# An early-fusion network with an LSTM on one core: output rows kept as (sequence, pair of steps), stored in rows of 2 KB

## The chip, the core and the metric

The kernel runs on one core of a Trainium2 chip. The metric is the device time of one execution in microseconds (us). A core has five engines that run at once and wait for each other on semaphores: TensorE (PE; its weight loads are shown apart as PEld), VectorE (DVE), ScalarE (ACT), GpSimd (POOL) and SyncE (SP). SP issues most transfers (queue q1 of the profile), ACT a few (q10), GpSimd the indirect ones (q0); all are carried out by the same 16 DMA engines. On-chip memory (SBUF) has 128 partitions; HBM is off the chip.

## The reference, cut to what matters

16 images become 441 tokens each, and 128 text tokens are appended: h has 16 sequences of 569 tokens of 256 numbers. Two layers follow. The second half of the second layer is what the change touches:

```python
h = h + _L1_attn_ref(_layernorm(h), ...)
h = h + _L1_ffn_ref(_layernorm(h), ...)

def _L1_ffn_ref(x, W_ih, W_hh, b_ih, b_hh, W_lin, b_lin, fw_att, bw_att):
    lstm_out = _lstm(x, W_ih, W_hh, b_ih, b_hh)        # 569 steps, 16 sequences, 256 units
    logits = lstm_out @ W_lin.T + b_lin
    g = argmax(logits, axis=-1)[..., None]             # 0 or 1 for each token
    w = g * lstm_out
    inc = jnp.cumsum(w, axis=1)                        # over the steps
    prefix = inc - w
    suffix = inc[:, -1:, :] - inc
    return 2.0 * lstm_out + prefix * fw_att + suffix * bw_att
```

Everything is float32. The output is (16, 569, 256): 9.32 MB, of which one token of one sequence is 1 KB. The suffix needs the total over all steps, which is known only after the last one.

## The kernel before, in words

**Stages.** First the tokenizer, the window attention and the routing (to about 900 us of the profile), then the experts of the mixture (to 1650), then layer 1. In layer 1 the attention of later tokens runs beside the recurrence of earlier ones (1650 to about 3250 us); then the recurrence runs alone (to 3443), and a tail follows.

**Order of the work.** The order on PE, DVE, ACT and POOL is fixed when the kernel is built. A planner (`Order.run`) takes streams of work, Python generators that yield an engine and an estimated time ("DVE+", 0.14 + ...) ahead of each instruction, and picks the next by these estimates; the recurrence (`steps`) is its chain and goes first. SP's transfers stand in the order in which the generators issue them. The change leaves all these estimates as they are.

**Rows between the attention and the LSTM.** `back` (L1390) ends each block of the attention by storing h into `HF` in HBM (L1489): one store for each sequence, 64 partitions of 1 KB for a block of 64 tokens. There are ten blocks (`BLOCKS`: 32 tokens, eight times 64, then 25). `HF[j]` is laid out (token, sequence, 256).

**The recurrence.** `steps` (L1576) does 569 steps. In each, TensorE adds W_hh times the state to the gates (L1637), ACT and DVE turn gates into the new state X (L1653 to L1680), which is kept with the units on the partitions: X is (128, 2 halves, step, sequence), its step 32 numbers apart because two copies of the 16 sequences stand side by side.

**The sums.** 37 runs (`RUNS`) of mostly 16 steps, then 8 and 1, go through `sums_of` (L1687) when their steps are done. It issues the load `hf` of the rows of h (L1692); computes the gate for all of a run's tokens (`fin`, L1700) and w (L1714) as (sequence, step); sums over the steps of each sequence by a scan (L1722, `sum`); makes `y`, laid out (step, sequence), from the sum, w and X in four DVE operations, two for each half of the units (L1729, L1734); turns y by TensorE so that tokens stand on the partitions (`turned`, L1743: eight steps x 16 sequences fill 128 partitions and make a unit; a run of 16 steps has two units); and adds hf (L1752). The sum goes to `PD` in HBM (L1757) as long as SBUF has no room, and later straight into `O`, an SBUF tile of (128, 72 units, 256), which first takes back what `PD` holds (L1789). So partition 16 t + b of O holds sequence b, and column u holds step 8 u + t.

**The tail.** The total of all steps, times bw_att, is spread over 128 partitions (L1797), turned (L1804) and copied to `T1` (L1806). T1 is added to all columns of O, in seven pieces of 2, 5, 8, 12, 14, 15 and 15 columns (L1810; L1815 for the last step alone). After each piece eight stores, one for each t, go out (L1818), in turn from SP and ACT: each reads 16 partitions, one for each sequence, and writes pieces of 1 KB that lie 8 KB apart in a sequence of the output.

Of the kernel before, what the change touches and what calls it, by code (L numbers as in the profile page):

```python
# [10 lines left out]
F32 = mybir.dt.float32  # L11
BF16 = mybir.dt.bfloat16
AF = mybir.ActivationFunctionType
ALU = mybir.AluOpType
# [3 lines left out]
D = 256  # L18
T = 569
# [30 lines left out]
BLOCKS = [(0, 32)] + [(32 + 64 * i, 64) for i in range(8)] + [(544, 25)]  # L50
STEPS = 8
UNITS_OF = [[(u, min(STEPS, n - u)) for u in range(0, n, STEPS)] for _, n in BLOCKS]

RUNS = []
# [228 lines left out]
def kernel(ctx: ExitStack, tc: tile.TileContext, a: dict, out: bass.AP):  # L283
    nc = tc.nc
    NB = out.shape[0]
# [3 lines left out]
    ident = const.tile([128, 128], F32, name="ident")  # L289
# [41 lines left out]
    dram = ctx.enter_context(tc.tile_pool(name="dram", bufs=1, space=bass.MemoryType.DRAM))  # L331
# [10 lines left out]
    before = route.tile([128, E, E], F32, name="before")  # L342
# [579 lines left out]


    HB = [dram.tile([128, D], F32, name=f"HB{p}") for p in range(NP)]
    HF = [dram.tile([n, NB, D], F32, name=f"HF{j}") for j, (_, n) in enumerate(BLOCKS)]

    XPD = [dram.tile([n, 2, NB, 512], F32, name=f"XPD{j}") for j, (_, n) in enumerate(BLOCKS)]
    PHD = dram.tile([128, 2, NP * 128], F32, name="PHD")
# [3 lines left out]
    ls = ctx.enter_context(tc.tile_pool(name="lstm", bufs=1))  # L932
# [14 lines left out]
    weights = ls.tile([128, 3, 2], F32, name="weights")  # L947
# [25 lines left out]
    with tc.tile_pool(name="lb", bufs=1) as lbp:  # L973
# [4 lines left out]
        v = lstm_b.rearrange("p (q r) -> p q r", r=128)[:, :, 64:96]  # L978
# [21 lines left out]
    def gate_columns(w, gate):  # L1000
        return w.rearrange("p (q r) -> p q r", r=128)[:, :, 32 * gate : 32 * gate + 32]

    for k in range(2):
        for gate in (0, 1, 3):
            v = gate_columns(Whh[:, k, :], gate)
# [5 lines left out]
    for v in (Wih[:, 0, :], Wih[:, 1, :]):  # L1011
        v = gate_columns(v, 2)
# [4 lines left out]
    for n in ("Wk2", "Wq2"):  # L1017
        t = l1w.tile([128, 2, 2, 64], F32, name=n)
# [10 lines left out]
    def bank(name, slot):  # L1029
        return ps.tile([128, 512], F32, name=name, tag=f"bank{slot}", bufs=1)  # L1030
# [359 lines left out]
    def back(p, c, batch, at, slot, late=False):  # L1390

        u = f"{p}_{c}_{late}"
# [6 lines left out]
        n = 1 if c8 else 2  # L1399
        block, r0, m = (len(BLOCKS) - 1, 0, 25) if late else (0, 32, 32) if c8 else (1 + c, 0, 64)  # L1400
# [8 lines left out]
        w = wk.tile([128, 2, 128], F32, name=f"w{u}", tag=f"w{slot}")  # L1409
# [22 lines left out]
        if c8:  # L1432
            h = wk.tile([128, n, D], F32, name=f"bh{u}", tag=f"bh{slot}")
            yield "at", ("kept", p, c)
            for j in range(2):
                for s in range(2):
                    b = 2 * j + s
# [5 lines left out]
        r = bank(f"r{u}", slot).rearrange("p (k n) -> p k n", k=2)  # L1443
# [16 lines left out]
        for k in range(2):  # L1460
            yield ("DVE/ACT", 0.34, 0.36) if c8 else ("DVE/ACT", 0.54, 0.46)
            src, to = tr[:, k, :], nT[:, k, :]
            if c8:
                src = src.rearrange("p (b x) -> p b x", x=64)[:, :, r0 : r0 + 32]
# [20 lines left out]
        for j in range(2):  # L1485
            for s in range(2):
                b = 2 * j + s
                src = h[32 * b : 32 * b + m, 0, :] if c8 else h[64 * s : 64 * s + m, j, :]
                nc.sync.dma_start(HF[block][:, 2 * p + b, :], src)  # L1489
        mv, rstd = yield from stats(h, f"d{u}", slot)  # L1490
        xn = yield from norm(h, mv, rstd, f"dxn{u}", slot)
        tr = yield from turn(xn, f"dtr{u}", slot, n)
# [3 lines left out]
        for i in range(2 * n):  # L1496
            j, half = i // 2, i % 2
# [74 lines left out]
    tail = {"stored": 0, "at": 0}  # L1572
# [114 lines left out]
    def sums_of(r, j, u, n, X):  # L1687


        m, units = NB * min(n, STEPS), -(-n // STEPS)  # L1690
        hf = ls.tile([128, 2, D], F32, name=f"hf{r}", tag="hf", bufs=3)
        nc.sync.dma_start(  # L1692
            hf[:m, :units, :],
            HF[j][u : u + n].rearrange("(i t) b d -> (t b) i d", i=units),
        )
        logit = ps.tile([128, 512], F32, name=f"fin{r}", tag="fin", bufs=1)
        logit = logit[:, : NB * n]
        for k in range(2):
            yield "PE", NB * n * COLUMN
            nc.tensor.matmul(  # L1700
                logit.rearrange("p (t b) -> p t b", b=NB), wl[:, k, :], X[:, k],
                start=(k == 0), stop=(k == 1),
            )

        w = ls.tile([128, 2, NB, n + 1], F32, name=f"w{r}", tag="w2", bufs=1)
        yield "ACT", 0.2
        if r:
            m_, before = sums[r - 1]
            nc.scalar.copy(w[:, :, :, 0], before[:, :, :, m_])
        else:  # L1710
            nc.scalar.activation(w[:, :, :, 0], X[:, :, 0, :], AF.Identity, scale=0.0)
        for k in range(2):
            yield "DVE", 0.14 + 0.002 * NB * n
            nc.vector.scalar_tensor_tensor(  # L1714
                w[:, k, :, 1:].rearrange("p b t -> p t b"),
                logit.rearrange("p (t b) -> p t b", b=NB), shut, X[:, k], ALU.is_gt, ALU.mult,
            )
        before = ls.tile([128, 2, NB, n + 1], F32, name=f"sum{r}", tag="sum", bufs=2)
        sums[r] = n, before
        for k in range(2):  # L1720
            yield "DVE+", 0.1 + 0.0025 * NB * (n + 1)
            nc.vector.tensor_tensor_scan(  # L1722
                before[:, k].rearrange("p b t -> p (b t)"), begins[n],
                w[:, k].rearrange("p b t -> p (b t)"), 0.0, ALU.mult, ALU.add,
            )
        y = ls.tile([128, 2, n, NB], F32, name=f"y{r}", tag="y", bufs=1)
        for k in range(2):
            yield "DVE+", 0.14 + 0.0022 * NB * n
            nc.vector.scalar_tensor_tensor(  # L1729
                y[:, k], before[:, k, :, :n].rearrange("p b t -> p t b"), weights[:, 0, k : k + 1],  # L1730
                X[:, k], ALU.mult, ALU.add,
            )
            yield "DVE+", 0.14 + 0.0022 * NB * n
            nc.vector.scalar_tensor_tensor(  # L1734
                y[:, k], w[:, k, :, 1:].rearrange("p b t -> p t b"), weights[:, 1, k : k + 1],
                y[:, k], ALU.mult, ALU.add,
            )
        turned = ps.tile([128, 512], F32, name=f"turned{r}", tag="fin", bufs=1)
        turned = turned.rearrange("p (i k x) -> p i k x", i=2, k=2)
        for i in range(units):  # L1740
            for k in range(2):
                yield "PE", TURN
                nc.tensor.transpose(  # L1743
                    turned[:m, i, k, :],
                    y[:, k, STEPS * i : STEPS * i + m // NB, :].rearrange("p t b -> p (t b)"), ident,
                )
        yield "DVE", 0.69 if units > 1 else 0.42
        o = hf[:, :units, :]
        if "O" in tail:
            o = tail["O"][:, tail["at"] : tail["at"] + units, :]  # L1750
        for i in range(units):
            nc.vector.tensor_tensor(  # L1752
                by_q(o[:m, i, :]), turned[:m, i].rearrange("p k (q x) -> p q k x", q=4),
                by_q(hf[:m, i, :]), ALU.add,
            )
        if "O" not in tail:
            nc.sync.dma_start(PD[:, tail["at"] : tail["at"] + units, :], o)  # L1757
            tail["stored"] += units
        tail["at"] += units

    def by_q(v):
        return v.rearrange("p (q k x) -> p q k x", q=4, k=2)
# [7 lines left out]
    with tc.manual_schedule(engines=ENGINES):  # L1770
# [10 lines left out]
        chain, rest = Stream(steps(), True), Stream(all_sums())  # L1781
# [3 lines left out]
        op = ctx.enter_context(tc.tile_pool(name="out", bufs=1))  # L1785
        tail["O"] = op.tile([128, sum(map(len, UNITS_OF)), D], F32, name="O")
        for u in range(0, tail["stored"], 8):
            u1 = min(u + 8, tail["stored"])
# [3 lines left out]


    n, total = sums[len(RUNS) - 1]
    all_rows = op.tile([128, 2, STEPS, NB], F32, name="all_rows")
    for k in range(2):
        nc.vector.tensor_scalar(  # L1797
            all_rows[:, k], total[:, k, :, n].unsqueeze(1).to_broadcast([128, STEPS, NB]),
            weights[:, 2, k : k + 1], None, ALU.mult,
        )  # L1800
    last = ps.tile([128, 512], F32, name="last", tag="fin", bufs=1)
    last = last[:, :D].rearrange("p (k x) -> p k x", k=2)
    for k in range(2):
        nc.tensor.transpose(last[:, k, :], all_rows[:, k].rearrange("p t b -> p (t b)"), ident)  # L1804
    T1 = op.tile([128, D], F32, name="T1")
    nc.vector.tensor_copy(by_q(T1), last.rearrange("p k (q x) -> p q k x", q=4))  # L1806
    O, full = tail["O"], T // STEPS
    for u0, u1 in ((0, 2), (2, 7), (7, 15), (15, 27), (27, 41), (41, 56), (56, full + 1)):
        k = min(u1, full)
        nc.vector.tensor_tensor(  # L1810
            O[:, u0:k, :], O[:, u0:k, :], T1.unsqueeze(1).to_broadcast([128, k - u0, D]), ALU.add
        )
        if u1 > full:
            rest = O[: NB * (T - full * STEPS), full, :]
            nc.vector.tensor_tensor(rest, rest, T1[: NB * (T - full * STEPS)], ALU.add)  # L1815
        for t in range(STEPS):
            n = u1 - u0 - (u1 > full and t >= T - full * STEPS)
            (nc.sync, nc.scalar)[t % 2].dma_start(  # L1818
                out[:, u0 * STEPS + t : (u0 + n - 1) * STEPS + t + 1 : STEPS, :],
                O[NB * t : NB * t + NB, u0 : u0 + n, :],  # L1820
            )


def layouts(i):
# [114 lines left out]
```

## Time and profile before

| | us |
|---|---|
| median of three runs (3497.92 to 3504.68) | 3501.64 |
| the profiled execution | 3500.74 |
| its span, first to last instruction | 3498.9 |
| PE busy / DVE busy / ACT busy | 3160.7 / 1958.2 / 1229.8 |
| layer 1 with attention and recurrence | about 1600 |
| recurrence alone | about 193 |
| end of the recurrence to the first add of T1 (3443 to 3452.5) | 9.5 |
| first add of T1 to the end | 46.4 |

How to read it: the span is what the trace covers; the execution's time is 1.8 us longer. Lines of groups give the line of the code, the engine, the operation, what is written and read, the shapes and the count, then busy us in all, the mean of one in ns, and the idle time of the engine ahead of them with what ended it. Lines of a timeline begin with the start and the duration in us; a bracket at their end is the idle time just before and what ended it. "x4" is a number of instructions.

### The profile page before, as it was taken

Reading aid. Unit: us, or ns where it says so; the run is one execution under the profiler, and the core shown is the slowest. Engines: PE = TensorE matmul, PEld = TensorE weight load, DVE = VectorE, ACT = ScalarE, POOL = GpSimd, SP = SyncE. Lnnn points to the kernel's source line nnn. Section 1 sums busy time; section 2 is a strip of 40 time slices with the busy share of each in tenths; the row PEclk is TensorE's granted clock in tenths of the full one; section 3 lists DMA queues with packets and bytes.
Section 4 is the critical chain, followed back from the end, with each engine's and each line's share of the span. In section 5 each row is a group of like instructions: output and inputs, shape, how many; then the busy total and the mean of one; then the engine's idle time right before and its main releaser. Section 6 shows DMA issues by size and latency. Waiting matters only on the chain.

```text
span 3498.9 us, 91880 instructions
## 1 busy us (share of the span) xinstructions
PE 3160.7 (90%) x37356; PEld 2388.9 (68%) x37356; DVE 1958.2 (56%) x6420; ACT 1229.8 (35%) x3914; POOL 767.2 (22%) x1343
## 2 busy tenths in 40 slices
PE   6999999899659999996799999999999999999873
PEld 4666666666448888885677777777777777776542
DVE  4677677776621111113466666666676666666444
ACT  3555455544212222222433333333333333322220
POOL 1253455435610000003412111111112221001000
PEclk9999999999779999998999999999999999999996
DMA  4121222101266666662323222232232222231304
GB/s 172 51 68 42 74 82 80 37 22 39 97 229 231 223 230 223 228 215 75 110 63 90 82 85 79 84 86 83 78 86 80 73 77 79 69 107 60 127 29 108
DMA packets 186903, 363.17 MB, mean 104 GB/s; under 512 B 25600, under 2 KB 120880, under 8 KB 173424
## 3 DMA queue, kind: packets, MB, share of 16 engines
q1 hardware_dynamic: 164448, 310.04, 28.1%
q0 software_dynamic: 13824, 37.77, 3.4%
q10 hardware_dynamic: 8208, 9.48, 0.9%
q8 instruction: 295, 4.83, 0.6%
q14 instruction: 128, 1.05, 0.1%
HBM read 238.87 MB, written 118.33 MB: 102 GB/s over the span
## 4 chain that ended last, share of the span: by engine, by line
PE 43%; DVE 5%; ACT 3%; POOL 2%; issue 1%; DMA 1%; DVEq 0%; SPq 0%; ACTq 0%; POOLq 0%
PE g L1637 16%; PE xm_False L1503 7%; PE g L1602 3%; PE eq L1297 2%; PE z L1328 2%; PE ek L1297 2%; PE v L1317 2%; PE po_False L1473 2%; PE ds_False L1378 1%; PE fin L1700 1%; ACT act L1653 1%; DVE ab L1659 1%; PE r_False L1446 1%; ACT th L1678 1%; DVE cT L1672 1%
## 5 line engine op out<-in xcount | busy, mean ns | idle before, releaser
L1637 PE MATMUL g<-W_hh,X 128*16 128x128 f32 (+1 forms) x18176 | 606.6, 274 | 70.0 <-DVE X L1680 68.7
L1637 PEld LDWEIGHTS g<-W_hh,X 128*16 128x16 f32 (+1 forms) x18176 | 454.2, 103 | 242.6 <-DVE X L1680 194.1
L1653 ACT ACTIVATE act<-g 128x96 f32<-128x96 f32 x568 | 142.5, 251 | 658.2 <-PE g L1637 656.8
L1659 DVE SCALAR_TENSOR_TENSOR ab<-act 128x64 f32<-128x64 f32 x568 | 127.7, 225 | 383.9 <-ACT act L1653 379.3
L1167 PE MATMUL y<-w,hT 128*128 128x256 f32 x1264 | 289.9, 382 | 6.3 <-ACT hT L1160 2.5
L1269 POOL DMA_INDIRECT yg<-YS,yat x144 | 147.8, 1026 | 662.5 <-DMA YS<-ys 626.0
L1160 ACT ACTIVATE hT<-hp,w 128x256 f32<-128x256 f32 x316 | 132.5, 472 | 456.2 <-PE hp L1153 293.3
L1153 PE MATMUL hp<-xt,w 128*128 128x256 f32 x1264 | 285.7, 379 | 0.0
L1503 PE MATMUL xm_False<-W_ih,dxT_False 128*128 128x256 f32 x1088 | 282.0, 393 | 1.7 <-ACT dxT_False L1189 1.1
L1167 PEld LDWEIGHTS y<-w,hT 128*128 128x128 f32 x1264 | 236.7, 190 | 46.8 <-ACT hT L1160 16.1
L1153 PEld LDWEIGHTS hp<-xt,w 128*128 128x128 f32 x1264 | 238.8, 190 | 33.9
L1678 ACT ACTIVATE th<-cT 128x32 f32<-128x32 f32 x569 | 130.4, 229 | 371.7 <-DVE toT L1675 367.5
L1173 DVE TENSOR_TENSOR ys<-y,w 128x512 f32<-128x512 f32 x79 | 54.6, 691 | 357.9 <-PE y L1167 357.9
L1602 PE MATMUL g<-xp,ident 128*32 128x128 f32 x4552 | 231.0, 275 | 8.3 <-DMA xp<-XPD 8.3
L1503 PEld LDWEIGHTS xm_False<-W_ih,dxT_False 128*128 128x128 f32 x1088 | 193.4, 190 | 51.2 <-issue 26.6
L1212 POOL TENSOR_SCALAR r_False_rstd<-r_False_mv,cols 128x2 f32<-128x2 f32 x36 | 14.4, 400 | 785.5 <-DVE r_False_mv L1207 785.1
L1680 DVE SCALAR_TENSOR_TENSOR X<-toT,th 128x32 f32<-128x32 f32 x569 | 109.1, 192 | 116.6 <-ACT th L1678 114.8
L883 POOL DMA_INDIRECT XS<-XN,at x144 | 150.5, 1045 | 38.8 <-issue 24.6
L674 PE MATMUL wqk<-wxT,wqkv 128*128 128x128 f32 x1152 | 152.0, 280 | 6.2 <-ACT wxT L668 5.9
L674 PEld LDWEIGHTS wqk<-wxT,wqkv 128*128 128x128 f32 x1152 | 141.6, 194 | 21.8 <-ACT wxT L668 12.2
L1602 PEld LDWEIGHTS g<-xp,ident 128*32 128x32 f32 x4552 | 128.7, 110 | 38.9 <-issue 29.5
L1145 DVE COPY xt<-xtr 128x512 f32<-128x512 f32 x79 | 51.0, 686 | 159.0 <-PE xtr L1140 159.0
(341 smaller groups left out, 6022.0 us busy)
## 6 DMA issues: line engine op xcount, KB each, us to landing
w<-in_wpack SPq DMA_DIRECT2D x79, 1154.0 KB
xp<-XPD SPq DMA_DIRECT2D x71, 512.0 KB
XPD<-xp_False SPq DMA_DIRECT2D x256, 128.0 KB
taps<-in_taps SPq DMA_DIRECT2D x16, 1764.0 KB
xs<-XS SPq DMA_DIRECT2D x79, 256.0 KB
YS<-ys SPq DMA_DIRECT2D x79, 256.0 KB
HD<-h SPq DMA_DIRECT2D x72, 128.0 KB
fh<-HD SPq DMA_DIRECT2D x72, 128.0 KB
```

Source lines behind the costliest of these rows:

```text
L674: nc.tensor.matmul(qk[:, j, m, :], wqkv[:, k, D * j + 128 * m : D * j + 128 * m + 128], xT[:, k, :], start=(k == 0), stop=(k == 1),)
L883: fill(0, nc.gpsimd.indirect_dma_start(out=XS[0], out_offset=bass.IndirectOffsetOnAxis(ap=at[:, i, c - lo : c - lo + 1], axis=0), in_=XN[p ...
L1153: nc.tensor.matmul(hp[:, i, :], w1[:, k, hc * 128 : (hc + 1) * 128], xT[:, k, :], start=(k == 0), stop=(k == 1),)
L1167: nc.tensor.matmul(y[:, i, :], hT[:, hc, 128 * i : 128 * i + 128], w2[:, hc, :], start=(hc == 0), stop=(hc == 3),)
L1269: nc.gpsimd.indirect_dma_start(out=y, out_offset=None, in_=YS[g], in_offset=bass.IndirectOffsetOnAxis(ap=yat[:, p + j, i, c : c + 1], axis=0),
L1297: nc.tensor.matmul(e[:, oc, :], l1[f"W{name}1"][:, k, oc * 128 : (oc + 1) * 128], xT[:, k, :], start=(k == 0), stop=(k == 1),)
L1503: nc.tensor.matmul(mm[:, 256 * part : 256 * part + 256], xT[:, k, j * 128 : (j + 1) * 128], Wih[:, k, at_ : at_ + 256], start=(k == 0), st ...
L1602: nc.tensor.matmul(g[32 * q : 32 * q + 32, :128], ident[:, 32 * (t % 4) : 32 * (t % 4) + 32], xp[:, t // 4, 128 * q : 128 * q + 128], star ...
L1637: nc.tensor.matmul(g[32 * q : 32 * q + NB * (1 + half), :128], before[:, kk, NB * (1 - half) :], Whh[:, kk, 512 * half + 128 * q : 512 * h ...
L1653: nc.scalar.activation(act[:, :96], g[:, :96], AF.Tanh, scale=0.5)
L1659: nc.vector.scalar_tensor_tensor(ab, act[:, :64].rearrange("p (g x) -> p g x", g=2), 1.0, act[:, 64:].rearrange("p (g x) -> p g x", g=2), ...
L1678: nc.scalar.activation(th.rearrange("p k x -> p (k x)"), cT, AF.Tanh, scale=0.5)
```

## The change

The rows of h and of the output are kept by (sequence, pair of steps). `HF[j]` becomes (sequence, token, 256). y becomes (sequence, step), so that the sum and w are read in their own order and X with its steps and sequences exchanged. A run of 16 steps is now turned in two halves by the parity of the step: unit i takes the steps 2 t + i, so the transposes read every second number of y. Partition 8 b + t then holds, in two neighbouring columns, steps 2 t and 2 t + 1 of sequence b: 2 KB that are contiguous in the output and in HF. The new function `by_rows` gives the matching view of HF for the load of hf and of the output for the stores. `PD`, its stores and loads have the same shapes as before.

In the tail, T1 is laid out by (sequence, step) too, and the last step alone, which has one row for each sequence, gets its own 16 rows by two more transposes and a small copy. T1 is added in 12 pieces of 2, 2, 4, 4, 4, six times 8, and 7 columns, and the output goes out in 37 stores, one for each run, in turn from SP and ACT: 35 of 128 partitions x 2 KB, one of 128 x 1 KB and one of 16 x 1 KB. In the changed kernel L1729 and L1734 become L1727 and L1732, L1743 becomes L1740, L1810 becomes L1820 and L1818 becomes L1824.

```diff
-    HF = [dram.tile([n, NB, D], F32, name=f"HF{j}") for j, (_, n) in enumerate(BLOCKS)]
+    HF = [dram.tile([NB, n, D], F32, name=f"HF{j}") for j, (_, n) in enumerate(BLOCKS)]
...
-                nc.sync.dma_start(HF[block][:, 2 * p + b, :], src)
+                nc.sync.dma_start(HF[block][2 * p + b], src)
...
-        nc.sync.dma_start(
-            hf[:m, :units, :],
-            HF[j][u : u + n].rearrange("(i t) b d -> (t b) i d", i=units),
-        )
+        nc.sync.dma_start(hf[:m, :units, :].rearrange("p i d -> p (i d)"), by_rows(HF[j], u, n))
...
-        y = ls.tile([128, 2, n, NB], F32, name=f"y{r}", tag="y", bufs=1)
+        y = ls.tile([128, 2, NB, n], F32, name=f"y{r}", tag="y", bufs=1)
...
-                y[:, k], before[:, k, :, :n].rearrange("p b t -> p t b"), weights[:, 0, k : k + 1],
-                X[:, k], ALU.mult, ALU.add,
+                y[:, k], before[:, k, :, :n], weights[:, 0, k : k + 1],
+                X[:, k].rearrange("p t b -> p b t"), ALU.mult, ALU.add,
...
-                y[:, k], w[:, k, :, 1:].rearrange("p b t -> p t b"), weights[:, 1, k : k + 1],
-                y[:, k], ALU.mult, ALU.add,
+                y[:, k], w[:, k, :, 1:], weights[:, 1, k : k + 1], y[:, k], ALU.mult, ALU.add,
...
-                    y[:, k, STEPS * i : STEPS * i + m // NB, :].rearrange("p t b -> p (t b)"), ident,
+                    y[:, k].rearrange("p b (t i) -> p i (b t)", i=units)[:, i, :], ident,
...
+    def by_rows(v, u, n):
+
+        v = v[:, u : u + n, :]
+        return v if n <= STEPS else v.rearrange("b (t i) d -> b t (i d)", i=n // STEPS)
...
-    all_rows = op.tile([128, 2, STEPS, NB], F32, name="all_rows")
+    all_rows = op.tile([128, 2, NB, STEPS], F32, name="all_rows")
...
+    for k in range(2):
+        nc.tensor.transpose(last[:NB, 1, k, :], all_rows[:, k, :, 0], ident)
     T1 = op.tile([128, D], F32, name="T1")
-    nc.vector.tensor_copy(by_q(T1), last.rearrange("p k (q x) -> p q k x", q=4))
-    O, full = tail["O"], T // STEPS
-    for u0, u1 in ((0, 2), (2, 7), (7, 15), (15, 27), (27, 41), (41, 56), (56, full + 1)):
-        k = min(u1, full)
-        nc.vector.tensor_tensor(
-            O[:, u0:k, :], O[:, u0:k, :], T1.unsqueeze(1).to_broadcast([128, k - u0, D]), ALU.add
+    nc.vector.tensor_copy(by_q(T1), last[:, 0].rearrange("p k (q x) -> p q k x", q=4))
+    O, at, done = tail["O"], 0, 0
+    for r, (j, u, n) in enumerate(RUNS):
+        units, t0 = -(-n // STEPS), BLOCKS[j][0] + u
+        if n == 1:
+            nc.vector.tensor_copy(by_q(T1[:NB]), last[:NB, 1].rearrange("p k (q x) -> p q k x", q=4))
+            nc.vector.tensor_tensor(O[:NB, at, :], O[:NB, at, :], T1[:NB], ALU.add)
+        elif at == done:
+            done = min(at + (2 if at < 4 else 4 if at < 16 else 8), sum(-(-n // STEPS) for _, _, n in RUNS if n > 1))
+            nc.vector.tensor_tensor(
+                O[:, at:done, :], O[:, at:done, :],
+                T1.unsqueeze(1).to_broadcast([128, done - at, D]), ALU.add,
+            )
+        (nc.sync, nc.scalar)[r % 2].dma_start(
+            by_rows(out, t0, n),
+            O[: NB * min(n, STEPS), at : at + units, :].rearrange("p i d -> p (i d)"),
         )
-        if u1 > full:
-            rest = O[: NB * (T - full * STEPS), full, :]
-            nc.vector.tensor_tensor(rest, rest, T1[: NB * (T - full * STEPS)], ALU.add)
-        for t in range(STEPS):
-            n = u1 - u0 - (u1 > full and t >= T - full * STEPS)
-            (nc.sync, nc.scalar)[t % 2].dma_start(
-                out[:, u0 * STEPS + t : (u0 + n - 1) * STEPS + t + 1 : STEPS, :],
-                O[NB * t : NB * t + NB, u0 : u0 + n, :],
-            )
+        at += units
```

More of the change, by code (lines that the diff above doesn't have):

```diff
@@ L1794 @@
     n, total = sums[len(RUNS) - 1]
-    all_rows = op.tile([128, 2, STEPS, NB], F32, name="all_rows")
+    all_rows = op.tile([128, 2, NB, STEPS], F32, name="all_rows")
     for k in range(2):
         nc.vector.tensor_scalar(
-            all_rows[:, k], total[:, k, :, n].unsqueeze(1).to_broadcast([128, STEPS, NB]),
+            all_rows[:, k], total[:, k, :, n].unsqueeze(2).to_broadcast([128, NB, STEPS]),
             weights[:, 2, k : k + 1], None, ALU.mult,
@@ L1801 @@
     last = ps.tile([128, 512], F32, name="last", tag="fin", bufs=1)
-    last = last[:, :D].rearrange("p (k x) -> p k x", k=2)
+    last = last.rearrange("p (i k x) -> p i k x", i=2, k=2)
     for k in range(2):
-        nc.tensor.transpose(last[:, k, :], all_rows[:, k].rearrange("p t b -> p (t b)"), ident)
+        nc.tensor.transpose(last[:, 0, k, :], all_rows[:, k].rearrange("p b t -> p (b t)"), ident)
+    for k in range(2):
+        nc.tensor.transpose(last[:NB, 1, k, :], all_rows[:, k, :, 0], ident)
     T1 = op.tile([128, D], F32, name="T1")
-    nc.vector.tensor_copy(by_q(T1), last.rearrange("p k (q x) -> p q k x", q=4))
-    O, full = tail["O"], T // STEPS
-    for u0, u1 in ((0, 2), (2, 7), (7, 15), (15, 27), (27, 41), (41, 56), (56, full + 1)):
-        k = min(u1, full)
-        nc.vector.tensor_tensor(
-            O[:, u0:k, :], O[:, u0:k, :], T1.unsqueeze(1).to_broadcast([128, k - u0, D]), ALU.add
-        )
-        if u1 > full:
-            rest = O[: NB * (T - full * STEPS), full, :]
-            nc.vector.tensor_tensor(rest, rest, T1[: NB * (T - full * STEPS)], ALU.add)
-        for t in range(STEPS):
-            n = u1 - u0 - (u1 > full and t >= T - full * STEPS)
-            (nc.sync, nc.scalar)[t % 2].dma_start(
-                out[:, u0 * STEPS + t : (u0 + n - 1) * STEPS + t + 1 : STEPS, :],
-                O[NB * t : NB * t + NB, u0 : u0 + n, :],
-            )
+    nc.vector.tensor_copy(by_q(T1), last[:, 0].rearrange("p k (q x) -> p q k x", q=4))
[14 more added lines that the diff above has]
+            O[: NB * min(n, STEPS), at : at + units, :].rearrange("p i d -> p (i d)"),
+        )
+        at += units
 def layouts(i):
```

## The prediction, made before the changed kernel was run

> **What bounds the kernel now.** I read the table by stage first (busy time of each engine; its last two columns are the share of time in which the 16 DMA engines are busy, and GB/s).
>
> ```profile
> 1650.00:3250.00 1600.00, 1539.10 (x24177) 1170.47 (x24179) 1053.12 (x4011) 592.82 (x2139) 308.56 (x542) 0.99 0.29 81
> 3250.00:3443.00 193.00, 151.76 (x3004) 93.38 (x2992) 90.61 (x401) 40.80 (x217) 0.00 (x0) 1.00 0.18 66
> 3443.00:3452.50 9.50, 3.41 (x10) 1.76 (x10) 6.34 (x26) 0.48 (x2) 0.00 (x0) 0.62 0.00 1
> 3452.50:3498.90 46.40, 0.00 (x0) 0.00 (x0) 19.82 (x8) 0.00 (x0) 0.00 (x0) 0.50 0.88 201
> ```
>
> From 1650 to 3443 us the recurrence sets the time: TensorE is busy 96% while it shares the core with the attention, then 79%; DMA is at 0.29 and 0.18. The edits in `sums_of` fall here. The last 46.4 us are different: TensorE does nothing, VectorE stops after 20 us, and the DMA engines are busy to the end. Only there can a transfer be the bound. The DMA view of 3453 to 3499 (packets, MB; then per queue: packets, MB, share of 16 engines over the 46 us):
>
> ```profile
> DMA packets 10001, 9.33 MB, mean 203 GB/s; under 512 B 896, under 2 KB 10000, under 8 KB 10000
> q1 hardware_dynamic: 5008, 4.67, 57.2%
> q10 hardware_dynamic: 4992, 4.65, 31.5%
> ```
>
> 9104 packets carry 1 KB each (896 are completion marks). (57.2 + 31.5)% x 46 us x 16 = 653 us of packet time; with some 9 us for the marks taken off (10 ns each), 644 / 9104 = 70.7 ns per KB, or 40.3 us on each of 16 engines. Is that what a store costs? Two stores that ran alone say no. First the view of 3211.1 to 3212 us, a store of `PD`, 128 partitions x 2 KB; then 3157.5 to 3159.3 us, two stores of `XPD`, each 64 partitions x 2 KB:
>
> ```profile
> DMA packets 143, 0.26 MB, mean 291 GB/s; under 512 B 15, under 2 KB 15, under 8 KB 143
> q1 hardware_dynamic: 143, 0.26, 74.5%
> ...
> DMA packets 160, 0.26 MB, mean 146 GB/s; under 512 B 32, under 2 KB 32, under 8 KB 160
> q1 hardware_dynamic: 160, 0.26, 63.7%
> ```
>
> 74.5% x 0.9 us x 16 / 128 = 84 ns for 2 KB from 128 partitions; 63.7% x 1.8 x 16 / 128 = 143 ns (141 without the marks) for the same 2 KB from 64. Which partitions a DMA reads thus decides its rate, and the tail's 70.7 ns per KB is the slow rate: 141 for 2 KB.
>
> [...] A store of the tail reads 16 partitions[...]; the trace has 203 on average and 204 to 241 in the 5 us windows. [...] No run here shows a store with 128 partitions on one side and 16 sequences on the other.
>
> **The change, part by part.** Built, both kernels have the same instructions in the same order, with the same waits, on every engine up to the tail; only shapes and strides differ. So I cost durations only.
>
> 1. `HF` with the sequence outermost: as many stores, 64 rows of 1 KB, now contiguous. [...] The `hf` load becomes 128 rows of 2 KB for 256 of 1 KB: at most 8 x 84 = 0.67 or 8 x 141 = 1.1 us of each engine. The last was issued at 3389.9 and is wanted at 3450.8, and DMA is at 0.18: nothing. Without that cover it would cost the landing of one load, some 2 us a run.
>
> 2. `y` by sequence. Durations by shape (VectorE, then the weight load of the transposes):
>
> ```profile
> L1734 DVE SCALAR_TENSOR_TENSOR y<-w,weights,y 128x256 f32<-128x256 f32 x70 | 45.2, 646 | 0.8
> L1729 DVE SCALAR_TENSOR_TENSOR y<-sum,weights,X 128x256 f32<-128x256 f32 x70 | 44.9, 641 | 0.0
> L1280 DVE SCALAR_TENSOR_TENSOR fh<-yg,share,fh 128x256 f32<-128x256 f32 x144 | 68.2, 477 | 12.5 <-DMA yg<-YS,yat 11.9
> L1743 PEld LDWEIGHTS turned<-ident,y 128*128 128x128 f32 x142 | 15.9, 141 | 9.5 <-issue 4.8 <-DVE y L1734 3.8
> ```
>
> L1280 is the same operation with all operands contiguous. L1734 becomes contiguous: 646 to 477 ns, 70 x 0.17 = 12 us less of VectorE. L1729 keeps one strided operand (X in place of the sum): 641 stays; bounds 477 and, if X's wider step is worse, some 900. Worth on the path: nothing. The timeline around such a pair shows why:
>
> ```profile
> 3430.16 0.64 DVE L1729 SCALAR_TENSOR_TENSOR y<-sum,weights,X 128x256 f32<-128x256 f32 x1
> ...
> 3430.84 0.65 DVE L1734 SCALAR_TENSOR_TENSOR y<-w,weights,y 128x256 f32<-128x256 f32 x1
> ...
> 3431.72 0.23 DVE L1659 SCALAR_TENSOR_TENSOR ab<-act 128x64 f32<-128x64 f32 x1 [0.23 <-ACT act L1653]
> ```
>
> After the pair VectorE idles 0.23 us for ACT: a shorter pair makes it idle longer. If L1729 grew by over 0.23 us, the rest would reach the recurrence (0.03 x 70, 2 us).
>
> 3. The transposes read `y` with a step of two elements as the stationary operand. No row shows a stepped weight load. [...] I take 141 ns unchanged; bounds nothing and doubled (the second rival). A gain is excluded: the read was contiguous.
>
> 4. The tail. Two more transposes of 16 columns stand before the copy of T1: the pair L1743 of that shape took 0.87 us with its waits; here they wait for nothing and follow a pair of 0.66: +0.3 us if the copy waits for all four, 0 if not; I take 0.3. The contiguous L1734 of 128 columns gives some 0.2 back. Adds: 12 in place of 7; by the rows of L1810 (0.69 us for 512 elements, 4.15 for 3840: 0.15 + 1.04 ns each) 20.7 us for 20.0, then 0.6 for the last step. They hide under the transfers. Issues: 37 for 56, some 0.34 us each (a `PD` store took 0.34): 6 us on each queue, hidden too. Transfers: 35 stores of 128 x 2 KB, one of 128 x 1 KB, one of 16 x 1 KB: 4480 packets of 2 KB, 144 of 1 KB (0.6 us per engine).
>
> What a 2 KB packet will take is the question. [...] 84 ns, 4480 x 84 / 16 = 23.5 us. [...] 141 ns, 39.5 us. [...] **I take the middle**[...]: 112 ns, 31.4 us[...].
>
> Of the tail's 46.4 us, 40.8 were DMA busy (88.7% of 46, marks included) and 5.6 the first add, issue, landing and gaps, which stay. After: 31.4 + 0.6 + 5.6 + 0.3 + some 0.4 of waits for the first small adds = 38.3. **Gain 8.1 us.** Against its own time, 3500.74 (span 3498.9 and 1.8 around it), that is 3492.6; the median shown is 0.9 higher: 3501.64 - 8.1 = 3493.5.
>
> **The rivals.** [...] For it: the `PD` store's 84 ns. Against: it has 128 rows on both sides. 23.5 + 0.6 + 5.6 + 0.3 = 30.0, and VectorE now is nearly the bound: its last 1792 elements are ready at 20.7 us, 4 stores still follow; I add 0.9: 30.9. Gain 15.5, 3486.1.
>
> [...] 39.5 + 0.6 + 5.6 + 0.3 = 46.0: 3501.2, no change[...].
>
> *Stepped weight loads cost double.* +0.14 us on each of 142. Four come in a row; in the recurrence alone TensorE then waits 0.31 us for X, so 0.25 of 0.56 shows, in the shared stage nearly all: 30 x 0.56 + 5 x 0.25 = 18 us. With the middle tail 3493.5 + 18 = 3511.5, slower. Decides from 8.1 / 142 = 57 ns per load on.
>
> **How the numbers follow.** Middle 0.42 (3488 to 3499 itself)[...], stepped loads 0.08. 0.2%, about what a measurement here can tell from no change, is 7 us. Faster by more: 0.6 of the middle[...], 0.25 + 0.31 = 0.56. Slower: 0.08. Same: the rest, 0.36. The range goes from the second case, less 3 us of spread as the three runs show, to the third: 3483 to 3502.
>
> **What would show it.** Right: 2 KB packets in the tail near 112 ns, a tail of 38 us at 240 to 300 GB/s; L1732 (was L1734) near 0.48 us with ACT's wait longer by as much; weight loads of `turned` at 141. Packets of 84 make the first rival true, 141 the second. Wrong altogether: 1650 to 3443 us changed in length by over 3 us.

## The result, and the profile after

The changed kernel takes 3487.55 us (median of six runs, 3484.45 to 3491.53); the kernel before, run beside it, 3501.55. The ratio is 0.9965, 95% interval 0.9954 to 0.9977: 14 us less, 8 to 16 by the interval. The prediction was 3493.5, a gain of 8.1.

The profiled execution took 3491.53 us with a span of 3489.8; it is the slowest of the six. Its table by stage, split as before and with the first add of T1 (3457.4) in the last row's stretch:

```profile
1650.00:3250.00 1600.00, 1538.78 (x24109) 1174.64 (x24124) 1044.36 (x4010) 592.38 (x2135) 308.44 (x546) 0.99 0.29 81
3250.00:3443.00 193.00, 152.34 (x2982) 94.28 (x2982) 90.91 (x404) 40.67 (x216) 0.00 (x0) 1.00 0.18 67
3443.00:3452.50 9.50, 5.13 (x82) 3.36 (x83) 5.00 (x20) 1.52 (x8) 0.00 (x0) 0.85 0.01 3
3452.50:3489.80 37.30, 2.47 (x9) 1.24 (x9) 23.16 (x26) 0.00 (x0) 0.00 (x0) 0.50 0.76 250
```

The rows of the recurrence are those of before, to 0.6 us of TensorE; VectorE has 9 us less to do from 1650 to 3250. The last row holds the end of the sums too: in this execution everything comes some 4 us later than in the one of before. That shift is not the change's. The first matmul of the recurrence starts at 1744.9 where it started at 1740.9, ahead of all computing in `sums_of`; from it to the last one there are 1701.7 us, before 1701.0. A second profile of the same kernel (below) starts its recurrence at 1740.0 and has a span of 3484.4.

The gain is all in the tail: from the first add of T1 to the end 3489.8 - 3457.4 = 32.4 us, where it was 46.4. The DMA view of 3457.9 to 3489.8 (packets, MB; per queue packets, MB, share of 16 engines):

```profile
DMA packets 5216, 9.32 MB, mean 292 GB/s; under 512 B 592, under 2 KB 736, under 8 KB 5216
q1 hardware_dynamic: 2624, 4.74, 44.3%
q10 hardware_dynamic: 2592, 4.59, 44.2%
```

The engines are as busy as before, 88.5%, but for a shorter time: 28.2 us each. 4480 packets carry 2 KB; their records in the trace have a mean of 98 ns, a median of 84, and one in ten is over 155. So most packets now run as fast as the lone `PD` store's (84 ns) and some as slow as the `XPD` stores' (141). Before, the mean was 70.8 ns for 1 KB, 142 for 2 KB. That mean hides two unlike queues: SP's packets of 1 KB took 91 ns on average and ACT's 50, with 46 for the median of all. (The lines of the prediction show it: q1 is busy for 57.2% and q10 for 31.5%, with the same bytes.) Now the two are alike, 97 and 100 ns for 2 KB.

The groups of y and its transposes:

```profile
L1740 PEld LDWEIGHTS turned<-ident,y 128*128 128x128 f32 x142 | 20.5, 206 | 8.8 <-issue 4.7 <-DVE y L1732 3.6
L1727 DVE SCALAR_TENSOR_TENSOR y<-sum,weights,X 128x256 f32<-128x256 f32 x70 | 46.5, 664 | 0.0
L1732 DVE SCALAR_TENSOR_TENSOR y<-w,weights,y 128x256 f32<-128x256 f32 x70 | 33.7, 481 | 0.8
```

The weight loads grew from 141 to 206 ns; the second DVE operation fell from 646 to 481, as L1280's 477 had said; the first went from 641 to 664. Little of it reaches the end: the recurrence as a whole is 0.7 us longer in this trace. The timeline of a step of the recurrence with all three in it, near 3436 us:

```profile
3435.52 0.48 DVE L1732 SCALAR_TENSOR_TENSOR y<-w,weights,y 128x256 f32<-128x256 f32 x1
3436.36 0.22 DVE L1659 SCALAR_TENSOR_TENSOR ab<-act 128x64 f32<-128x64 f32 x1 [0.35 <-ACT act L1653]
3436.93 0.55 PEld L1740 LDWEIGHTS turned<-ident,y 128*128 128x128 f32 x4 [0.20 <-issue]
...
3437.66 0.80 PEld L1637 LDWEIGHTS g<-W_hh,X 128*16 128x16 f32 x32 [0.18 <-DVE X L1680]
```

VectorE now waits 0.35 us for ACT where it waited 0.23. TensorE waits 0.18 us for X after the four transposes; before, the same line had 0.31:

```profile
3433.01 0.80 PEld L1637 LDWEIGHTS g<-W_hh,X 128*16 128x16 f32 x32 [0.31 <-DVE X L1680]
```

So the loads have used up 0.13 us of a wait that was there, and 0.18 is left.

One small loss is on the path. The copy of T1 waits for the two added transposes:

```profile
3456.93 0.42 DVE L1811 COPY T<-last 128x256 f32<-128x256 f32 x1 [1.23 <-PE last L1809]
```

Before, the wait there was 0.80 us, so 0.43 us are lost:

```profile
3452.03 0.42 DVE L1806 COPY T<-last 128x256 f32<-128x256 f32 x1 [0.80 <-PE last L1804]
```

### The profile page after: what moved, and what is told of

Its sections match the earlier page's. It is cut to its first block, busy times and chain, and to the rows that moved or that the text cites. A ratio compares the mean times of both kernels' runs of the same rounds, so it can differ in the third digit from the quotient of the medians.

```text
span 3489.8 us, 91861 instructions
## 1 busy us (share of the span) xinstructions
PE 3166.0 (91%) x37341; PEld 2398.4 (69%) x37358; DVE 1949.9 (56%) x6426; ACT 1228.8 (35%) x3914; POOL 764.0 (22%) x1343
## 4 chain that ended last, share of the span: by engine, by line
PE 43%; DVE 5%; ACT 3%; POOL 2%; issue 1%; DMA 0%; SPq 0%; DVEq 0%; ACTq 0%; POOLq 0%
PE g L1637 16%; PE xm_False L1503 7%; PE g L1602 3%; PE eq L1297 2%; PE z L1328 2%; PE ek L1297 2%; PE v L1317 2%; PE po_False L1473 2%; PE ds_False L1378 1%; PE fin L1698 1%; PE r_False L1446 1%; ACT act L1653 1%; DVE ab L1659 1%; ACT th L1678 1%; DVE cT L1672 1%
## 5 line engine op out<-in xcount | busy, mean ns | idle before, releaser
L1167 PEld LDWEIGHTS y<-w,hT 128*128 128x128 f32 x1264 | 237.1, 190 | 46.4 <-ACT hT L1160 16.0
```

Source lines behind the costliest of these rows:

```text
L1167: nc.tensor.matmul(y[:, i, :], hT[:, hc, 128 * i : 128 * i + 128], w2[:, hc, :], start=(hc == 0), stop=(hc == 3),)
```

## The experiments

Theory: the time of a packet in the tail depends on which partitions the stores in flight read, and the change spreads each store over all 128. Rivals: the 2 KB packets make it faster; or the smaller number of stores does. Beside that: is the price of the stepped weight loads really hidden, and why is the mean 98 ns and not 84 or 141? In what follows, the tail is the time from the first add of T1 to the end. Four of the runs (stores in another order, 1 KB packets, whole units, and the first run of weight loads without a step) were measured beside a kernel before that took 3593.97 us; most of the difference is in the recurrence (1781 and 1783 us, for 1701, in the two of them that share its code up to the tail), for a reason that is not known. They are compared by ratios and by their tails. The kernel before was not profiled beside them, but the two tails that can be compared, the changed kernel's 32.4 and the 31.8 us of the run without a step, which has the same stores, agree.

**Stores in another order.** Each pair of stores, one from SP and one from ACT, reads groups of 16 partitions that lie 32 apart; before, they lay 16 apart. The kernel before with

```diff
-        for t in range(STEPS):
+        for at, t in enumerate((0, 2, 1, 3, 4, 6, 5, 7)):
...
-            (nc.sync, nc.scalar)[t % 2].dma_start(
+            (nc.sync, nc.scalar)[at % 2].dma_start(
```

> The kernel before with one edit: in the tail the steps t go out in the order 0, 2, 1, 3, 4, 6, 5, 7[...]. Same packets, same number of stores. [...] 9.32 MB take 80 us, packets near 140 ns per KB, the kernel about 3540 us. If small packets or the number of stores bound it, nothing changes: 3501 us, 71 ns per KB.

Measured: 3601.31 us, ratio 1.0020 (1.0012 to 1.0029), tail 56.1 us. DMA view of the tail, 3540 to 3595.6:

```profile
DMA packets 10001, 9.33 MB, mean 168 GB/s; under 512 B 896, under 2 KB 10000, under 8 KB 10000
q10 hardware_dynamic: 4992, 4.65, 43.0%
q1 hardware_dynamic: 5008, 4.67, 40.1%
```

The order of the same stores costs 10 us of tail (7 us of the whole time, 4 to 10 by the interval), which neither size nor number of stores explains. But it is a quarter of what I had estimated from this theory: 80 ns a packet, against 70.8 in the kernel before and 140 forecast.

**The same 16 partitions for all stores.** The kernel before with

```diff
-                O[NB * t : NB * t + NB, u0 : u0 + n, :],
+                O[:NB, u0 : u0 + n, :],
```

> The kernel before with every store of the tail reading partitions 0 to 15 of O, whatever its step: same stores, same packets, same places in the output, but the rows of the other steps are left out (each row of eight gets the first one's data). [...] the tail takes some 80 + 6 = 86 us, packets 141 ns per KB, the kernel 3541 us.[...]

Measured: 3559.85 us beside 3501.5, ratio 1.0168 (1.0147 to 1.0188), tail 105.7 us. DMA view, 3454.6 to 3559.8:

```profile
DMA packets 10001, 9.33 MB, mean 89 GB/s; under 512 B 896, under 2 KB 10000, under 8 KB 10000
q1 hardware_dynamic: 5008, 4.67, 41.8%
q10 hardware_dynamic: 4992, 4.65, 41.7%
```

The steady part, 3500 to 3520 us (the last two columns are the DMA share and GB/s):

```profile
3500.00:3520.00 20.00, 0.00 (x0) 0.00 (x0) 0.00 (x0) 0.00 (x0) 0.00 (x0) 0.50 0.89 94
```

With every store on partitions 0 to 15 the rate is 94 GB/s; the packets of 1 KB take 153 ns and fill 89% of the engines' time. Only the partitions that are read differ from the kernel before (203 GB/s, 70.8 ns), so they set the rate; the 141 ns on record were an estimate, and too low. The stores in another order, whose pairs are 32 partitions apart, ran at 168, between the two. The kernel before, whose two queues read different groups of 16, moved 203, a little more than twice 94. How a packet is held up when stores read the same partitions is not shown: the trace doesn't name the engine of a packet.

**The same partitions in 1 KB packets.** The changed kernel with

```diff
-        (nc.sync, nc.scalar)[r % 2].dma_start(
-            by_rows(out, t0, n),
-            O[: NB * min(n, STEPS), at : at + units, :].rearrange("p i d -> p (i d)"),
-        )
+        rows = out[:, t0 : t0 + n, :].rearrange("b (t i) d -> b t i d", i=units)
+        for i in range(units):
+            (nc.sync, nc.scalar)[r % 2].dma_start(
+                rows[:, :, i, :], O[: NB * min(n, STEPS), at + i, :]
+            )
```

> The changed kernel, each store of 128 partitions x 2 KB cut in two of 128 partitions x 1 KB (even steps, odd steps): 1 KB packets and twice the stores, the same partitions. [...] packets take 47 to 52 ns, the tail 32 to 35 us, the kernel 3487 to 3491 us. If the 2 KB rows are what it gained, packets take 65 to 71 ns, the tail 42 to 46 us, the kernel 3497 to 3502 us.

Measured: 3579.39 us, ratio 0.9959 (0.9943 to 0.9974), tail 34.8 us. DMA view, 3541.2 to 3575.5:

```profile
DMA packets 10257, 9.34 MB, mean 272 GB/s; under 512 B 1152, under 2 KB 10256, under 8 KB 10256
q1 hardware_dynamic: 5216, 4.74, 44.7%
q10 hardware_dynamic: 5040, 4.59, 43.2%
```

52 ns a packet of 1 KB, against 70.8 before and 49 (half of 98) in the changed kernel. Of the tail's 14.0 us, 11.6 come with the spread over partitions and 2.4 with the 2 KB rows and the smaller number of stores. (The places in HBM, 2 KB apart in place of 8, change with the spread, and no run separates the two on this side; that the partitions alone can set the rate, the run on the same 16 shows: 153 ns against 70.8.)

**Whole units, steps outermost.** The kernel before, its stores replaced by

```diff
+        for u in range(u0, u1):
+            m = min(STEPS, T - u * STEPS)
+            (nc.sync, nc.scalar)[u % 2].dma_start(
+                out[:, u * STEPS : u * STEPS + m, :].rearrange("b t d -> t b d"), O[: NB * m, u, :]
+            )
```

> The kernel before with its layout of O (partition 16 t + b) but one store of 128 partitions for each column, outermost dimension 8 steps on the side of the output: 72 stores of 1 KB packets. [...] tail 55 to 60 us, kernel 3510 to 3516 us; engine loads uneven in the DMA view (share near 0.5). If only the spread over all 128 partitions counts, the tail is as short as the changed kernel's, 32 to 35 us, and the kernel 3488 us.

Measured: 3599.62 us, ratio 1.0018 (1.0011 to 1.0025), tail 54.0 us. DMA view, 3544.1 to 3597.6, with its row of busy tenths in 40 slices:

```profile
DMA  0455555555555555555555555555555555555520
DMA packets 9689, 9.33 MB, mean 174 GB/s; under 512 B 584, under 2 KB 9688, under 8 KB 9688
```

The 16 engines are busy for half of the time on average, at 47 ns a packet, close to the 46 that was the median in the kernel before. The trace shows the share of 0.5, not which engines. Reading all 128 partitions in packets of 1 KB is not enough: with 8 steps outermost on the output's side the share is 0.5, with the 16 sequences outermost, in the run before this one, it is 0.88 (the order of the rows in `O` differs too). To bring the sequences to the front is what the change of layout is for.

**The output's side.** The changed kernel with

```diff
-            by_rows(out, t0, n),
+            by_rows(out, t0, n) if n < 2 * STEPS else PD[:, at : at + units, :].rearrange("p i d -> p (i d)"),
```

> The changed kernel with the 35 stores of 128 x 2 KB sent to PD, a tensor in HBM with 128 rows, in place of the output; the output stays unwritten but for its last nine steps. The SBUF side, the packets of 2 KB, their number and the adds stay; only the other side has 128 rows in place of 16 sequences of 8 pairs. [...] packets go from 98 to 84 or 86 ns, the tail from 32.4 to 28 or 29 us, the kernel 3 to 4 us below the changed one. If the rest of 98 against 84 ns comes from two queues or from HBM, nothing changes.

Measured: tail 28.8 us; 3485.63 us beside 3501.99, ratio 0.9955 (0.9940 to 0.9971). DMA view, 3455.8 to 3484.1:

```profile
DMA packets 5216, 9.32 MB, mean 330 GB/s; under 512 B 592, under 2 KB 736, under 8 KB 5216
q1 hardware_dynamic: 2624, 4.74, 45.8%
q10 hardware_dynamic: 2592, 4.59, 44.7%
```

The records have 88.6 ns a packet, one in ten over 94 where it was 155. So with 128 rows on both sides the slow packets are nearly gone, and 3 us of the changed tail go with the 16 sequences on one side. Why is not shown: no trace names the engine of a packet, and the addresses in HBM differ too, which this run does not separate. The whole time can't show 3 us.

**One queue.** The changed kernel with all stores on SP:

```diff
-        (nc.sync, nc.scalar)[r % 2].dma_start(
+        nc.sync.dma_start(
```

> The changed kernel with all 37 stores on SP. [...] packets go from 98 towards 141 ns and the tail from 32 to 36 to 46 us. [...] packets stay near 98 ns and the tail near 32 us; SP's 37 issues of 0.34 to 0.55 us, 13 to 20 us in all, stay under the transfers.

Measured: 3487.87 us beside 3501.5, ratio 0.9964 (0.9950 to 0.9978), tail 32.5 us, 98 ns a packet. DMA view, 3451.8 to 3483.8:

```profile
DMA packets 5216, 9.32 MB, mean 291 GB/s; under 512 B 592, under 2 KB 736, under 8 KB 5216
q1 hardware_dynamic: 5216, 9.32, 88.1%
```

In the changed kernel the two queues play no part: 98 ns and 32.4 us with both, 98 and 32.5 with one.

**Weight loads without a step.** The changed kernel with

```diff
-        y = ls.tile([128, 2, NB, n], F32, name=f"y{r}", tag="y", bufs=1)
+        y = ls.tile([128, 2, units, NB, n // units], F32, name=f"y{r}", tag="y", bufs=1)
...
-                    y[:, k].rearrange("p b (t i) -> p i (b t)", i=units)[:, i, :], ident,
+                    y[:, k, i].rearrange("p b t -> p (b t)"), ident,
```

and the DVE operations writing `y[:, k].rearrange("p i b t -> p b t i")`.

> The changed kernel with y kept apart by parity (sequence and step of one unit contiguous), so that the weight loads of the transposes read without a step; the DVE operations write y with a step instead. In the trace of the changed kernel these loads take 206 ns against 141 before. Expected here: loads at 141 ns again, the DVE operations on y 0.64 us or a little more. If the longer loads were hidden, the time stays within 2 us of the changed kernel's 3487.5 us. If they were on the path, 142 x 0.065 = 9 us come back: 3478 us.

Measured: 3574.75 us beside 3593.97, ratio 0.9945 (0.9932 to 0.9959), which overlaps with the changed kernel's; loads 143 ns, the DVE operations 686 and 688. Its recurrence took 1777.1 us and that of the run in 1 KB packets, with stepped loads, 1784.7; but two runs beside it without stepped loads took 1781.0 and 1782.8. That and the interval are too wide to tell 2 us from none, so the same edit was run again beside the changed kernel, together with the two 16-column transposes moved behind the copy:

```diff
+    T1 = op.tile([128, D], F32, name="T1")
+    nc.vector.tensor_copy(by_q(T1), last[:, 0].rearrange("p k (q x) -> p q k x", q=4))
     for k in range(2):
         nc.tensor.transpose(last[:NB, 1, k, :], all_rows[:, k, :, 0], ident)
-    T1 = op.tile([128, D], F32, name="T1")
-    nc.vector.tensor_copy(by_q(T1), last[:, 0].rearrange("p k (q x) -> p q k x", q=4))
```

> The changed kernel with y apart by parity (weight loads without a step) and with the two 16-column transposes of the last step moved behind the copy of T1, which waited for them in the trace (0.42 us more than in the kernel before). Expected: the copy 0.4 us earlier, loads at 141 ns, the kernel 0.4 to 3 us below the changed one, which this measurement may not resolve.

> The changed kernel itself once more, as the measure for the other runs on this chip. Expected: the kernel before less 14 us (ratio 0.996), tail from the first add of T1 to the end 32.4 us, weight loads of the transposes 206 ns.

Measured together, with 3501.99 for the kernel before: 3487.67 (ratio 0.9958, 0.9945 to 0.9972) for the edited, 3487.30 (0.9959, 0.9945 to 0.9972) for the changed kernel. The edited kernel's groups and copy:

```profile
L1743 PEld LDWEIGHTS turned<-ident,y 128*128 128x128 f32 x142 | 15.9, 141 | 9.4 <-issue 4.8 <-DVE y L1733 3.6
L1733 DVE SCALAR_TENSOR_TENSOR y<-w,weights,y 128x256 f32<-128x256 f32 x70 | 48.2, 688 | 0.8
...
3452.85 0.42 DVE L1812 COPY T<-last 128x256 f32<-128x256 f32 x1 [0.80 <-PE last L1810]
```

Loads of 141 again, the copy's wait back at 0.80, and no difference in time that the medians can show. From the first to the last matmul of the recurrence there are 1701.0 us against 1702.0. In the traces at this speed it is 1701.0 in two with loads of 141 ns (the kernel before, this one) and 1701.7 to 1702.8 in four with stepped loads (205 to 208 ns), so some 1 us of the 9 us of longer loads shows and the rest is hidden. Had they all shown, the ratio here would be about 0.9933, outside this run's interval; the first run alone would have allowed it. (In this run the slower pair on VectorE uses up the wait for ACT, which could offset the shorter loads; but where the recurrence is alone a step with the transposes in it takes 2.71 to 2.72 us in both kernels, as does one without them, so there neither costs anything.) The tails, 31.7 and 31.8, are near the 32.4 of the first profile.

**A step of four.** The changed kernel with

```diff
-        y = ls.tile([128, 2, NB, n], F32, name=f"y{r}", tag="y", bufs=1)
+        y = ls.tile([128, NB, n, 2], F32, name=f"y{r}", tag="y", bufs=1)
```

and `y[:, :, :, k]` for `y[:, k]`.

> The changed kernel with the two halves of y interleaved, so that the weight loads of the transposes step by four numbers (16 bytes) where they stepped by two, and the DVE operations on y write every second number. Loads took 141 ns without a step and 206 with a step of two. [...] a step of four takes some 330 ns, four loads in a row 0.5 us more than now, which is over the 0.18 us that TensorE still waits for X: up to 0.3 x 37 = 11 us slower than the changed kernel. If a step costs the same whatever its size, loads stay at 206 ns and the time is that of the changed kernel.

Measured: 3486.59 us, ratio 0.9960 (0.9944 to 0.9975). The groups:

```profile
L1740 PEld LDWEIGHTS turned<-ident,y 128*128 128x128 f32 x142 | 20.8, 208 | 8.8 <-issue 4.8 <-DVE y L1732 3.6
L1732 DVE SCALAR_TENSOR_TENSOR y<-w,weights,y 128x256 f32<-128x256 f32 x70 | 33.8, 483 | 0.9
```

208 ns for a step of four, 206 for two: the 330 ns, an estimate of mine, were wrong. A step costs some 65 ns a load in both sizes. The DVE operation, with every second number of y read and written, stays at 483.

## Why the prediction was right in its direction and short in its size

*Where the gain lies*: right. The recurrence moved by 0.7 us (1.8 at most in the other traces), the tail by 14.0, and in the tail the DMA engines were the bound on both sides (busy 88.7% before, 88.5% after).

*Steps 1 and 2* (HF, hf, y on VectorE): right in being hidden; what the packets of hf take was not measured, but nothing waits for this load in either trace. L1732 is at 481 ns (0.48 forecast) and the wait for ACT grew, by 0.12 us. L1727 took 664, inside the bounds given, with 0.35 us of wait behind it.

*Step 3* (weight loads at 141): wrong in size. That a step of two costs nothing was my estimate, with no row to show it; the loads took 206. For VectorE it would have held: its step of two in the run with interleaved halves cost nothing (483 against 481). The mechanism of the rival with stepped weight loads was thus there, at 65 ns a load, above the 57 at which I had let it decide; it decided nothing, because I had counted nearly all of it as showing in the shared stage, and the runs show 0.7 to 1.8 us over the whole recurrence, with 0.13 us of slack used per run of steps where it is alone.

*Step 4, ahead of the adds*: +0.3 us forecast for the copy, 0.43 measured.

*Step 4, the transfers*: the term that was mis-sized. I took the middle of the `PD` store's 84 ns and the `XPD` stores' 141, 112 ns a packet, 31.4 us; that the truth would lie halfway was an estimate. It was 98, (98 - 84) / (141 - 84) = a quarter of the way, 27.4 us. That is 4.0 us, and another 0.2 is in the packets of 1 KB (0.4 us for 0.6). The gaps make some 1.4: 32.4 - 27.9 of packet time leaves 4.5 us now, 4.9 with the copy's delay, where I had 5.6 + 0.3 + 0.4 = 6.3; why they shrank was not looked into. Together that is about the 5.5 us by which the profiles' gain, 46.4 - 32.4 - 0.4 = 13.6, passes my 8.1. The medians have 14.0, which agrees with it within its interval. One more size was wrong and stayed hidden: an issue took 1.3 us in the median, not 0.34, which makes 22 and 23 us on the two queues.

*What misled me*: the mean of 70.7 ns. I read it as the slow rate of every packet, but it is that of SP's 91 ns and ACT's 50, and half of all packets took 46. So the tail before does not show that all its packets were held up alike, and why its two queues differ stays open. I had read it that way, and so took the packets of the changed kernel as slower than they are and kept 0.18 for 141 ns throughout, which nothing in the runs supports.

*The rival with 84 ns a packet*, to which I had given 0.32, was the nearest (3486.1, 1.5 us off, where my own number is 6 us off), but not for its reason: 98 were measured. The run into `PD` comes near that case, with 88.6 ns and a tail of 28.8 us, beside the changed kernel's 32.

## What to carry to other kernels

Ask of every store which partitions are read at the same moment, and what stands outermost on the other side. In these runs a packet of 1 KB took 153 ns when all stores read the same 16 partitions and 52 when each read 128; and stores of 128 partitions in such packets kept the engines busy for 0.5 of the time with 8 steps outermost in the output, for 0.88 with 16 sequences. In a stretch where only transfers run, a layout that gives 128 partitions and 16 rows at the front was worth more (11.6 us of 46) than doubling the packets and halving the number of stores (2.4). And a mean can hide two unlike queues (91 and 50 ns in 70.8): look at each queue's own packets, and pin the partitions in a run to see what they give.

## What the runs showed of the hardware that was not expected

A weight load of 128 columns took 141 ns from contiguous float32 and 206 to 208 with a step of two or four numbers. Stores that all read the same 16 partitions, in 1 KB packets, moved 94 GB/s. The stores of the kernel before, put in another order, moved 168 GB/s where they had moved 203. And in the kernel before, two queues with the same stores on other partitions were served unlike: 91 ns a packet for SP's, 50 for ACT's.
